# Three passes of 12-bit digits for v in three of the four linear-attention units

## The chip, the cores and the metric

The kernel runs on one core of one Trainium2 (trn2) chip, as one launch. The metric is the device time in microseconds, the median of several runs. Engines are named as the profile names them: PE is TensorE and PEld its weight loads, DVE is VectorE, ACT is ScalarE, POOL is GpSimd, SP is the queue that issues the DMAs.

## The reference, cut to what matters

Two transformer layers on a float32 tensor of 2 x 512 x 256. Only the third of the four blocks is touched:

```python
x = x + _layernorm(_L0_attn_ref(_layernorm(x), ...))   # 16 heads of 128, causal
x = x + _layernorm(_L0_ffn_ref(_layernorm(x), ...))    # 256 -> 2048 -> 256, 4-bit weights
x = x + _layernorm(_L1_attn_ref(_layernorm(x), ...))   # linear attention, below
x = x + _layernorm(_L1_ffn_ref(_layernorm(x), ...))    # 256 -> 688 -> 256, table weights

def _L1_attn_ref(x, W_qkv, W_out):        # D = 256, 16 heads of 16
    q, k, v = split(x @ W_qkv.T, 3)       # x: 2 x 512 x 256
    q, k = elu(q) + 1, elu(k) + 1
    kv_cumsum = cumsum(k * v, axis=sequence)
    k_cumsum = cumsum(k, axis=sequence)
    out = q * kv_cumsum / (q * k_cumsum + 1e-9)
    return out @ W_out.T * 16 ** -0.5
```

Everything is float32, the products on PE too.

## The kernel before, in words

The 1024 rows are four units of 256 rows (`NUNIT`, `TU`). First comes the attention of layer 0, head by head, up to about 384 us of the profile. Then the loop at the end of `sandwich_kernel` writes, for each unit u, the feed-forward block of layer 0: `ffn_hidden(u)` makes eight pairs of hidden chunks, each a gate half (four products into a bank of tag "mm") and an up half (four products into a bank of tag "s"), then a GELU on ACT and a product `hT` on DVE; `ffn_out(u)` multiplies by the down weights. Two halves of unit u+1 are written ahead of `ffn_out(u)`. After the last unit follow `silu_hidden` and `silu_out`, the second feed-forward block, unit by unit.

A product is one call of `matmul`, lines 278 to 286, a 128 x 128 stationary block against 256 moving columns. Since `halved[0]` is set early in the kernel, each call is written as two halves of 64 stationary columns, which run side by side in the array. The hardware runs a float32 half as two instructions (two weight loads and two matmuls in the records), so one call is four matmul records, and each record streams the 256 columns twice.

Beside this main line of PE work run chains: `after_ffn(u)` (norms, then `linear_attention(u)`) is a Python generator that yields a delay and is taken up again by `poll()` when `now[0]`, the planner's own clock of PE, has passed its due time. `poll()` is called after each half of `ffn_hidden` (1.73 us of PE work) and after each two chunks of `ffn_out` (0.86 us). `now[0]` grows by `matmul` calls alone. Each engine's instructions run in the order in which they were written, so the planner decides what stands behind what.

In `linear_attention(u)` the products of k, q and v are written in this order, with a `yield until(f)` after k and after q, so that one half of `ffn_hidden` lies between them. For units 0 to 2 this falls into `ffn_hidden(u + 1)`; unit 3 (`last`) runs inside the second feed-forward block and is on the way to the end.

DVE has filler work: `select_in` builds the down weights `wd` of the second feed-forward block by bit masks and selects, 19 steps a piece. Its steps wait in `vector.fills`; the wrapper `Engine.__getattr__` writes them into gaps that the planner sees in front of another DVE instruction that has to wait for data. `vector.flush()` writes what is left.

Of the kernel before, what the change touches and what calls it, by code (L numbers as in the profile page):

```python
# [10 lines left out]
F32 = mybir.dt.float32  # L11
I32 = mybir.dt.int32
F8 = mybir.dt.float8e4
U8 = mybir.dt.uint8
SIGN = 0x80808080 - (1 << 32)
REST3 = 0x1C1C1C1C
AF = mybir.ActivationFunctionType
ALU = mybir.AluOpType

P = 128  # L20
# [3 lines left out]
D = 256  # L24
NT = S // P
NK = D // P
# [8 lines left out]
TU = HT * P  # L35
NUNIT = B * NT // HT
TURNED = [P, 4, NK, HT, 32]
INTER = 688
NO = -(-INTER // P)
# [151 lines left out]
def sandwich_kernel(  # L191
# [26 lines left out]
    nc = tc.nc  # L218
# [10 lines left out]
    vector, scalar = Engine("DVE", nc.vector, times), Engine("ACT", nc.scalar, times)  # L229
    pool, sync = Engine("POOL", nc.gpsimd, times), Engine("SP", nc.sync, times)  # L230
# [3 lines left out]
    def bank(tag):  # L234
        tile = psum.tile([P, 512], F32, tag=tag, name=f"ps_{tag}")
        used = banks.setdefault(tag, deque(maxlen=2))
        if len(used) == 2:
            times.floor[tile.name] = times.end(used[0])
        used.append(tile.name)
        return tile  # L240
# [36 lines left out]
    def matmul(out, lhsT, rhs, start, stop, beside=False, **more):  # L277
        m = lhsT.shape[-1]
        step = HALF if halved[0] else P
        for at in range(0, m, step):  # L280
            part = slice(at, min(at + step, m))
            nc.tensor.matmul(out[part], lhsT=lhsT[:, part], rhs=rhs, start=start, stop=stop, **more)  # L282
        now[0] = max(now[0], times.start("PE", [out], [lhsT, rhs]))
        if not beside:
            now[0] += (math.prod(rhs.shape[1:]) / 0.6 + 5) / 1e3
        times.add("PE", now[0], [out], [lhsT, rhs])
# [33 lines left out]
    wd = w1.tile([P, NO, D], F32, name="wd")  # L320
# [16 lines left out]
    def chunk(t, kc):  # L337

        return t[:, :, kc].rearrange("p a j t -> p j a t")
# [71 lines left out]
    def norms(u, y, stage, to, eps=EPS, strided=False):  # L411

        x = [xs[u][:, j, :] for j in range(HT)]
        first = [stats(t, eps) for t in y]
        second = []
        for j in range(HT):
            yield until(first[j][0])
            add_scaled(x[j], y[j], first[j][0])  # L420
            second.append(stats(x[j], EPS))
        n = acts.tile([P, HT, D], F32, tag="ln", name=f"ln{stage}_{u}")
        for j in range(HT):
            rstd, shift = second[j]
            yield until(rstd, shift)
            to_n, from_x = n[:, j, :], x[j]
            if strided:
                to_n = to_n.rearrange("p (k m) -> p k m", k=NK)
                from_x = from_x.rearrange("p (m k) -> p k m", k=NK)
            scalar.activation(to_n, from_x, AF.Identity, bias=shift, scale=rstd)  # L430
        yield until(n)
        tr = turning(u, stage)
        for j in range(HT):
            turned_about(tr, n, j)
        brought(to, tr)
        for j in range(HT):
            scalar.activation(x[j], x[j], AF.Identity, bias=first[j][1])

        yield 0.0 if (u, stage) == (2, 1) else until(to)
# [93 lines left out]
    with ExitStack() as at:  # L533
# [257 lines left out]
        def dequantised(packed, scales, u, name, w):  # L791
# [12 lines left out]
            else:  # L804

                for half in range(2):
# [5 lines left out]
                    )  # L812
            p8 = dq.tile([P, UNIT], U8, tag="p8", name="p8")
            c8 = dq.tile([P, 2, UNIT], U8, tag="c8", name="c8")
            two, t = p8.bitcast(I32), pk[:, : UNIT // 4]
# [17 lines left out]
            def values():  # L833
                vector.scalar_tensor_tensor(
                    w,
                    c8.bitcast(F8),
                    64.0,
# [18 lines left out]
        scratch = fh.tile([P, 5, wg.shape[-1]], F32, tag="hT", name="scratch", bufs=1)  # L856
# [275 lines left out]
            yield  # L1132

        def after_ffn(u, po):
            xT2[u] = late["lp"].tile(TURNED, F32, tag="xT2", name=f"xT2_{u}", bufs=1)
            yield from norms(u, [po[:, j * D : (j + 1) * D] for j in range(HT)], 2, xT2[u])
            yield from linear_attention(u)

        xT2, late = {}, {}
# [136 lines left out]
        for rows, cs, base in (  # L1276
# [5 lines left out]
                out=mask[rows, cs],  # L1282
                in_=mask[rows, cs],
# [20 lines left out]
        for i in range(NS + 2):  # L1304
# [5 lines left out]
    lw = late["lw"] = ctx.enter_context(tc.tile_pool(name="lw", bufs=1))  # L1310
    lp = late["lp"] = ctx.enter_context(tc.tile_pool(name="lp", bufs=2))
# [4 lines left out]
    wqkv_sb = lw.tile([P, NK, 3 * D], F32, name="wqkv_sb")  # L1316
# [1 line left out]
    wout_sb = lw.tile([P, NK, D], F32, name="wout_sb")  # L1318
    sync.dma_start(out=wout_sb, in_=wout)
    carry = {}  # L1320
    scratch = lw.tile([P, 8, 2 * D], F32, name="scratch2")
    vector.flush()
    select_in(
        [scratch[:, j] for j in range(8)],
        [
            tuple(t[:, o : o + 2, :].rearrange("p o d -> p (o d)") for t in (down_i, wd))
            for o in range(0, NO, 2)
        ],
    )

    def linear_attention(u):
        def flat(t):
            return t.rearrange("p k t -> p (k t)")

        def project(part, tag):
            ps = bank(tag)
            for ch in range(NK):
                for kc in range(NK):
                    matmul(
                        ps[:, ch * TU : (ch + 1) * TU],  # L1340
                        wqkv_sb[:, kc, part * D + ch * P : part * D + (ch + 1) * P],
                        chunk(xT2[u], kc),
                        kc == 0,
                        kc == NK - 1,
                    )
            return ps

        def of(name, bufs=1):
            return lp.tile([P, NK, TU], F32, tag=name, name=f"{name}_{u}", bufs=bufs)

        k, q, v, ek, eq = of("k"), of("q"), of("v"), of("ek"), of("eq")

        last = u == NUNIT - 1
        for part, e, f in ((1, ek, k), (0, eq, q)):
            ps = project(part, "mm")
            scalar.activation(flat(e), ps, AF.Relu, scale=-1.0)
            scalar.activation(flat(f), ps, AF.Relu)
            if last:

                scalar.activation(e, e, AF.Exp, scale=-1.0)  # L1360
                vector.tensor_scalar(e, e, -1.0, 1.0, ALU.add, ALU.add)
                pool.tensor_add(f, f, e)
            else:
                yield until(f)
        ps = project(2, "s")
        scalar.copy(flat(v), ps)
        if not last:
            for e in (ek, eq):
                scalar.activation(e, e, AF.Exp, scale=-1.0)
            yield until(ek, eq)  # L1370
            for e, f in ((ek, k), (eq, q)):
                vector.tensor_scalar(e, e, -1.0, 1.0, ALU.add, ALU.add)
                pool.tensor_add(f, f, e)
        yield until(k, v)
        ks, kvs, den, lT = of("ks", 2), of("kvs", 2), of("den"), of("lT")

        def running_sum(to, of_):
            for ch in range(NK):
                before = carry[to is kvs, u - 1][:, ch, TU - 1 :] if u % 2 else 0.0
                vector.tensor_tensor_scan(  # L1380
                    to[:, ch, :], ones, of_[:, ch, :], before, ALU.mult, ALU.add
                )
            carry[to is kvs, u] = to

        running_sum(ks, k)
        if not last:
            yield until(ks, q)
        vector.tensor_mul(den, q, ks)
        vector.tensor_scalar(den, den, EPS_LIN, None, ALU.add)
        vector.tensor_mul(v, k, v)  # L1390
        yield until(v)
        running_sum(kvs, v)
        pool.tensor_mul(v, q, kvs)
        yield until(den)
        for ch in range(NK):
            for t in range(HT):
                part = ch, slice(t * P, (t + 1) * P)
                vector.reciprocal(den[:, *part], den[:, *part])
                pool.tensor_mul(lT[:, *part], v[:, *part], den[:, *part])
                yield 0.3  # L1400
        yield until(lT) - 0.8 if last else until(lT) + 0.5
        po = bank("t" if last else "o")
        for t in range(HT):
            for ch in range(NK):
                matmul(
                    po[:, t * D : (t + 1) * D],
                    lT[:, ch, t * P : (t + 1) * P],
                    wout_sb[:, ch, :],
                    ch == 0,
                    ch == NK - 1,  # L1410
                )
        yield 0.3
        t = gp.tile(TURNED, F32, tag="xT3", name=f"xT3_{u}", bufs=4)

        y = [po[:, j * D : (j + 1) * D] for j in range(HT)]
        yield from last_norms(u, y, t, 16 * EPS) if last else norms(u, y, 3, t, 16 * EPS)
        xT3[u] = t
# [221 lines left out]
```

## Time and profile before

| what | value |
|---|---|
| device time, median of 3 runs | 618.01 us (617.85 to 618.13) |
| span of the profiled execution, first to last instruction | 616.7 us |
| what lies around the span in the median of the runs (618.01 - 616.7) | 1.3 us |
| PE busy | 611.1 us, 99%, in 4968 matmul records |
| DVE busy | 486.2 us, 79% |
| ACT busy | 309.3 us, 50% |
| POOL busy | 277.1 us, 45% |
| granted TensorE clock, mean | 0.998 |

A row of the timeline gives the start and the length in us, the engine, the line, the operation, what it writes and reads, the shape and how many records were merged into the row; in brackets the idle time before it and what ended it. All PE rows bear line 282 and most others line 183, since helpers record them; the tiles tell them apart. A matmul record's end is modelled: of its 379 ns some 213 are streaming, so rows overlap, and the time from one row's start to the next row's start is what the stream costs.

### The profile page before, as it was taken

What the parts mean: (1) busy time and instruction counts of PE and PEld (TensorE: products, weight loads), DVE (VectorE), ACT (ScalarE), POOL (GpSimd) and SP (SyncE); (2) the same over time, 40 slices, a digit from 0 to 9 for tenths busy, and PEclk for the clock granted to TensorE, in tenths of its full rate; (3) what the DMA queues carried; (4) which work ended last, traced back from release to release, by engine and by line L of the source; (5) the groups of instructions that cost most, each with busy time, mean ns of one, the idle gap of its engine ahead of it and who ended that gap; (6) DMA issues with size and microseconds to landing.
All of it is one profiled execution on the core that took longest, in us unless ns stands there. A gap on an engine that the chain in (4) does not pass through costs nothing.

```text
span 616.7 us, 13347 instructions
## 1 busy us (share of the span) xinstructions
PE 611.1 (99%) x4968; PEld 470.2 (76%) x4968; DVE 486.2 (79%) x1169; ACT 309.3 (50%) x716; POOL 277.1 (45%) x346
## 2 busy tenths in 40 slices
PE   9999999999999999999999999999999999999996
PEld 7455556566676776767777899999999999996665
DVE  7989988887887999989899789869986751562963
ACT  6657776775666657676566651232324223325210
POOL 5355657454453575855667300350261350161531
PEclk9999999999999999999999999999999999999999
DMA  8477474765647547556552340211001000001010
GB/s 228 137 186 211 107 199 125 171 168 144 158 127 177 168 116 191 152 142 178 113 141 60 84 104 26 98 35 35 1 8 31 1 18 18 1 2 35 19 53 18
DMA packets 44463, 61.43 MB, mean 100 GB/s; under 512 B 5232, under 2 KB 32368, under 8 KB 44400
## 3 DMA queue, kind: packets, MB, share of 16 engines
q1 hardware_dynamic: 44400, 60.59, 38.0%
q8 instruction: 39, 0.64, 0.4%
q14 instruction: 24, 0.20, 0.1%
HBM read 28.59 MB, written 1.05 MB: 48 GB/s over the span
## 4 chain that ended last, share of the span: by engine, by line
PE 98%; DVE 1%; issue 0%; POOL 0%; DVEq 0%
PE ps_mm L282 40%; PE ps_o L282 22%; PE ps_s L282 21%; PE ps_t L282 14%; PE ps_o L579 1%; DVE x L183 0%; DVE p L183 0%; DVE rr L183 0%; DVE ra L183 0%; DVE centred L183 0%; POOL rstd L183 0%; DVE wg L183 0%; PE ps_t L289 0%; DVE st L183 0%; DVE st_last L183 0%
## 5 line engine op out<-in xcount | busy, mean ns | idle before, releaser
L183 DVE SCALAR_TENSOR_TENSOR rr<-ps_mm,cols_sb,sin_sb 64x512 f32<-64x512 f32 (+1 forms) x126 | 93.4, 741 | 3.6 <-PE ps_mm L282 0.7
L183 POOL TENSOR_TENSOR wg<-wg,scratch 128x752 f32<-128x752 f32 x30 | 53.8, 1794 | 89.3 <-DVE scratch L183 86.9
L282 PE MATMUL ps_mm<-xT,wg 128*64 128x256 f32 (+1 forms) x704 | 89.4, 379 | 0.0
L282 PE MATMUL ps_s<-xT,wu 128*64 128x256 f32 x672 | 85.4, 379 | 0.0
L183 ACT ACTIVATE p<-p,mn 128x512 f32<-128x512 f32 (+3 forms) x128 | 70.3, 550 | 27.6 <-DVE mn L183 27.6
L282 PE MATMUL ps_o<-wd,hT 128*64 128x256 f32 (+1 forms) x704 | 77.2, 375 | 0.0
L282 PE MATMUL ps_t<-pT,v 128*64 128x256 f32 (+3 forms) x512 | 76.1, 432 | 0.0
L282 PEld LDWEIGHTS ps_mm<-xT,wg 128*64 128x64 f32 (+1 forms) x704 | 71.7, 137 | 5.5 <-ACT si L183 0.4
L282 PEld LDWEIGHTS ps_o<-wd,hT 128*64 128x64 f32 x704 | 68.9, 137 | 6.2
L282 PEld LDWEIGHTS ps_s<-xT,wu 128*64 128x64 f32 x672 | 69.5, 137 | 4.5 <-DVE hT L183 0.3
L282 PEld LDWEIGHTS ps_t<-pT,v 128*64 128x64 f32 x512 | 49.7, 137 | 27.1 <-issue 19.0
L183 ACT ACTIVATE p<-p,rs 128x512 f32<-128x512 f32 (+3 forms) x128 | 61.4, 551 | 11.2 <-DVE rs L183 9.3
L282 PEld LDWEIGHTS ps_o<-wo,oT 128*64 128x64 f32 x512 | 49.9, 137 | 17.8 <-issue 13.3
L282 PE MATMUL ps_o<-wo,oT 128*64 128x256 f32 x512 | 62.5, 379 | 0.0
L282 PE MATMUL ps_mm<-xT,wq 128*64 128x512 f32 (+2 forms) x256 | 60.5, 577 | 0.1
L282 PE MATMUL ps_mm<-xT,wk 128*64 128x512 f32 x248 | 60.0, 592 | 0.0
L183 POOL TENSOR_TENSOR ra<-ra,cos_sb 128x512 f32<-128x512 f32 (+1 forms) x33 | 41.1, 1245 | 40.2 <-ACT ra L183 38.4
L282 PE MATMUL ps_s<-kT,qT 128*64 128x64 f32 (+5 forms) x384 | 57.0, 424 | 0.0
L282 PE MATMUL ps_mm<-wv,xTv 128*64 128x256 f32 x464 | 56.4, 379 | 0.0
L183 DVE STREAM_TRANSPOSE turned<-p 128x512 f32<-128x512 f32 (+3 forms) x128 | 54.1, 480 | 1.2 <-ACT p L183 0.2
L183 ACT ACTIVATE ln<-x,shift,rstd 128x256 f32<-128x256 f32 x22 | 13.3, 607 | 79.0 <-POOL shift L183 78.2
L282 PEld LDWEIGHTS ps_s<-kT,qT 128*64 128x64 f32 x384 | 34.6, 137 | 23.9 <-issue 11.6
(161 smaller groups left out, 965.3 us busy)
## 6 DMA issues: line engine op xcount, KB each, us to landing
pT<-turned SPq DMA_DIRECT2D x128, 208.0 KB, 3.9
wo<-in_wo SPq DMA_DIRECT2D x17, 256.0 KB, 4.2
wv<-in_wv SPq DMA_DIRECT2D x16, 256.0 KB, 4.2
wq<-in_wq SPq DMA_DIRECT2D x15, 256.0 KB, 4.2
wk<-in_wk SPq DMA_DIRECT2D x15, 256.0 KB, 4.0
xT<-tr SPq DMA_DIRECT2D x48, 64.0 KB, 2.1
pk_g<-in_gate_p SPq DMA_DIRECT2D x4, 256.0 KB, 4.6
sc_g<-in_gate_s SPq DMA_DIRECT2D x8, 128.0 KB, 4.2
```

The lines of the kernel that those rows point to most:

```text
L183: return write(*args, **more)
L282: nc.tensor.matmul(out[part], lhsT=lhsT[:, part], rhs=rhs, start=start, stop=stop, **more)
L579: nc.tensor.matmul(warm[:, :P], lhsT=units, rhs=units, start=True, stop=True)
```

## The change

In units 0 to 2, v's product is no longer four float32 calls but twelve matmuls with operands of type float32r, written straight to `nc.tensor.matmul`, over all 128 stationary columns. The operands are split into digits of 12 bits: x is a high part `top` and a low part, the weights likewise. Pass 0 takes the raw operands (wv3[0], xT2), pass 1 the low parts (the weights' times 4096), and pass 2 the differences. Between pass 1 and pass 2 ACT multiplies the sum in PSUM by 1 + 1/4096; the sum of the three is then the product of the whole numbers. Three DVE instructions per unit make `top`, the low part and the difference of x; four more, `split_weights`, make the weights' parts once, in unit 0. One more DMA copies the raw weights into wv3[0]. Between pass 1 and ACT's multiplication the chain yields 0.5. The bank is of tag "t" where it was "s". To make room, the scratch of `select_in` is halved: the down weights are made in six pieces of 256 columns, where there were three of 512. Unit 3 is as before.

```diff
@@ after_ffn
-            xT2[u] = late["lp"].tile(TURNED, F32, tag="xT2", name=f"xT2_{u}", bufs=1)
+            t = late["lp"].tile(TURNED, F32R, tag="xT2", name=f"xT2_{u}", bufs=1)
+            xT2[u] = t.bitcast(F32)
@@ ahead of linear_attention
-    scratch = lw.tile([P, 8, 2 * D], F32, name="scratch2")
+    scratch = lw.tile([P, 8, D], F32, name="scratch2")
     vector.flush()
     select_in(
         [scratch[:, j] for j in range(8)],
-        [
-            tuple(t[:, o : o + 2, :].rearrange("p o d -> p (o d)") for t in (down_i, wd))
-            for o in range(0, NO, 2)
-        ],
+        [(down_i[:, o, :], wd[:, o, :]) for o in range(0, NO)],
     )
+    wv3 = [lw.tile([P, NK, D], F32R, name=f"wv3_{n}") for n in range(3)]
+    wv_raw = wqkv_sb[:, :, 2 * D :]
+    sync.dma_start(out=wv3[0].bitcast(F32), in_=wv_raw)
+
+    def split_weights():
+        top = lp.tile([P, NK, TU], F32, tag="den", name="top_w", bufs=1)
+        low = lp.tile([P, NK, TU], F32, tag="lT", name="low_w", bufs=1)
+        vector.tensor_scalar(top.bitcast(I32), wv_raw.bitcast(I32), HIGH, None, ALU.bitwise_and)
+        vector.tensor_sub(low, wv_raw, top)
+        vector.tensor_scalar(wv3[1], low, DIGIT, None, ALU.mult)
+        vector.scalar_tensor_tensor(wv3[2], low, -DIGIT, top, ALU.mult, ALU.add)
@@ linear_attention
+        if u == 0:
+            split_weights()
         k, q, v, ek, eq = of("k"), of("q"), of("v"), of("ek"), of("eq")
...
-        ps = project(2, "s")
+        if last:
+            ps = project(2, "s")
+        else:
+            x3 = [xT2[u].bitcast(F32R), *(lp.tile(TURNED, F32R, tag=n, name=f"x{n}_{u}", bufs=1) for n in ("lT", "den"))]
+            top = lp.tile(TURNED, F32, tag="top", name=f"top_{u}", bufs=1)
+            vector.tensor_scalar(top.bitcast(I32), xT2[u].bitcast(I32), HIGH, None, ALU.bitwise_and)
+            vector.tensor_sub(x3[1], xT2[u], top)
+            vector.scalar_tensor_tensor(x3[2], top, -1.0 - 1.0 / DIGIT, xT2[u], ALU.mult, ALU.add)
+            ps = bank("t")
+            for n in (0, 1, 2):
+                if n == 2:
+                    yield 0.5
+                    scalar.mul(ps, ps, 1.0 + 1.0 / DIGIT)
+                for ch in range(NK):
+                    for kc in range(NK):
+                        nc.tensor.matmul(
+                            ps[:, ch * TU : (ch + 1) * TU],
+                            lhsT=wv3[n][:, kc, ch * P : (ch + 1) * P],
+                            rhs=chunk(x3[n], kc),
+                            start=n == 0 and ch == 0 and kc == 0,
+                            stop=n == 2 and kc == NK - 1,
+                            skip_group_check=True,
+                        )
         scalar.copy(flat(v), ps)
```

More of the change, by code (lines that the diff above doesn't have):

```diff
@@ L13 @@
 F8 = mybir.dt.float8e4
+F32R = mybir.dt.float32r
+HIGH = 0xFFFFF000 - (1 << 32)
+DIGIT = 4096.0
 U8 = mybir.dt.uint8
```

## The prediction

> **What bounds the kernel now.** I read the page first: busy shares and the chain that ended last.
>
> ```profile
> PE 611.1 (99%) x4968; PEld 470.2 (76%) x4968; DVE 486.2 (79%) x1169; ACT 309.3 (50%) x716; POOL 277.1 (45%) x346
> ...
> PE 98%; DVE 1%; issue 0%; POOL 0%; DVEq 0%
> ```
>
> PE is busy from end to end and is 98% of the chain. So a microsecond of PE work taken out anywhere is a microsecond of the end, as long as PE stays fed, and a microsecond in which PE waits is one lost. DVE, ACT and POOL matter only where PE would have to wait for them.
>
> Next, the PE timeline around the three changed products (ps_s<-xT,wqkv_sb; the ps_mm rows with wqkv_sb are k and q; wg and wu are gate and up halves of the feed-forward block).
>
> ```profile
> 426.76 2.00 PE L282 MATMUL ps_mm<-xT,wqkv_sb 128*64 128x256 f32 x16
> 428.49 2.01 PE L282 MATMUL ps_mm<-xT,wg 128*64 128x256 f32 x16
> 430.21 2.01 PE L282 MATMUL ps_s<-xT,wqkv_sb 128*64 128x256 f32 x16
> ...
> 471.65 2.01 PE L282 MATMUL ps_s<-xT,wu 128*64 128x256 f32 x16
> 473.38 2.00 PE L282 MATMUL ps_s<-xT,wqkv_sb 128*64 128x256 f32 x16
> 475.11 2.01 PE L282 MATMUL ps_mm<-xT,wg 128*64 128x256 f32 x16
> ...
> 521.73 2.01 PE L282 MATMUL ps_mm<-xT,wg 128*64 128x256 f32 x16
> 523.46 2.00 PE L282 MATMUL ps_s<-xT,wqkv_sb 128*64 128x256 f32 x16
> ```
>
> Two things are to be seen. Each row starts 1.73 us after the one before, with nothing between: v costs 1.73 us per unit today (16 records, 0.108 each). And in units 0 and 2 v stands behind a gate half (wg), in unit 1 behind an up half (wu). That decides below whether the digits are ready.
>
> **Passes removed and added.** Per unit four calls, 1.73 us, go. Twelve matmuls come, each over all 128 columns, in one pass if float32r is what the change takes it for. No row of before has this type. The nearest are the full-width float32 products at the start of the kernel:
>
> ```profile
> 7.48 0.61 PE L282 MATMUL ps_mm<-xT,wq 128*128 128x128 f32 x4
> 7.93 0.60 PE L282 MATMUL ps_o<-xT,wk 128*128 128x256 f32 x2
> 8.36 0.40 PE L289 MATMUL ps_t<-ident,n 128*128 128x128 f32 x2
> 8.60 0.60 PE L282 MATMUL ps_o<-xT,wk 128*128 128x256 f32 x2
> 9.19 0.44 PE L282 MATMUL ps_mm<-xT,wq 128*64 128x256 f32 x2
> ```
>
> A float32 record streams its columns twice. The four of 128 columns (256 streamed) take 0.45 us from 7.48 to 7.93, 0.11 each, with a load of 128 stationary columns hidden under each. Two records of 256 columns take 0.43 from 7.93 to 8.36, 0.215 each. A float32r matmul streams 256 columns once, so I take 0.11: 12 x 0.11 = 1.32 us. The upper end is 0.215, if this type streams twice as well: 2.58 us. Below 0.107, the 256 columns' share of these rows, nothing speaks for it. Gain: 1.73 - 1.32 = 0.41 per unit, 1.2 us in all. This is the most the change can bring: 0.2% of 618.0, which is about what a measurement of this kernel can tell from no change.
>
> **Switching between half and full width.** Every call around is two 64-column halves; the new matmuls take the whole array. Passes 0 and 1 are one block and pass 2, behind the yield, another: two blocks per unit, each with a switch in and one out, 12 switches in all. From full to half there is one row: the second of the two full-width records of the row at 8.60 starts 0.38 before that row's end, at 8.82, and the first half at 9.19. That is 0.37 us where 0.215 is streaming: 0.15 too much, and part of it was a wait for ACT's xT, which ended at 9.13. So this switch costs 0 to 0.15. From half to full no row exists. It lies between 0 (weights load under the last halves, as they do everywhere else) and 0.30: the 0.379 that a half's record lasts in its group less its 0.213 of streaming, 0.17, until the array is empty, and 0.137, the mean of the halves' loads, for a weight load that is no longer hidden. I take 0.10 and 0.15, nearer the middle than the free end, since the one row that has a switch shows a hole: 0.25 a pair, 6 pairs, 1.5 us; ends 0 and 2.7.
>
> The Trainium skill speaks against the change here: "TensorEngine Tiling (Array Packing)", Tiling Modes, says that a change of tiling mode, not of the tile alone, drains the engine. With the load time of "TensorE: Matmul & The Clock Gate", section LDWEIGHTS (columns divided by 1.2, in ns), 107 and 53 ns would be uncovered per pair, an estimate of 1.0 us over six pairs before the emptying itself. No row of before shows a change from half to full.
>
> **The wait of pass 1 for its digits.** Pass 1 needs `top` and the low part from DVE, and stands directly behind pass 0 in PE's queue, so everything on PE waits with it. On DVE the two are queued behind what was written last: the `hT` product of the last up half. Its rows for unit 1:
>
> ```profile
> 473.79 0.69 DVE L183 TENSOR_TENSOR hT<-ge,ps_s 128x512 f32<-128x512 f32 x1 [0.80 <-PE ps_s L282]
> 480.43 0.69 DVE L183 TENSOR_TENSOR hT<-ge,ps_s 128x512 f32<-128x512 f32 x1 [5.96 <-ACT ge L183]
> 481.03 0.42 DVE L183 TENSOR_SCALAR ek<-ek 128x512 f32<-128x512 f32 x1
> 481.37 0.42 DVE L183 TENSOR_SCALAR eq<-eq 128x512 f32<-128x512 f32 x1
> ```
>
> Where v stands behind an up half, hT can start only when that half has ended: 473.79, 0.41 after v could start on PE (473.38). From start to start an hT takes 0.60, an instruction on one tensor of this size 0.34 (481.03 to 481.37) and one on two about that of hT, 0.60. The low part is then there at 473.38 + 0.41 + 0.60 + 0.34 + 0.60 + 0.1 for the semaphore = 475.43. Pass 0 would be done at 473.38 + 0.15 + 0.44 = 473.97. PE waits 1.5 us. Where v stands behind a gate half (units 0 and 2), hT belongs to an up half further back: in unit 0 its row starts at 427.26, the low part is made by 428.9 with the same steps, and v starts at 430.21. That leaves over 1.2 us, in unit 2 (hT at 520.40, v at 523.46) 1.4; there the digits cost nothing.
>
> Does unit 1 keep its place? The chain of unit 0 no longer advances the planner's clock by v's 1.73 us, so later due times move against the halves. I followed the planner's due times by hand: unit 1's k comes due between a gate half and the up half after it, about 0.6 us behind the poll that would turn the order. So I take the order of before for unit 1 (odds two to one) and for unit 2 (three to two), and one wait: 1.5 us; ends 0 and 3.0.
>
> **ACT between passes.** A 512-wide multiplication in PSUM, at most the copy of v (0.59 us). The yield puts a half of 1.73 us on PE between, and ACT's queue there holds one GELU (0.60) that is ready: 1.2 us under 1.73. Nothing on the path. Without that half each unit would lose some 0.7.
>
> **DVE's further work.** Splitting the weights: four instructions, 0.34 + 0.60 + 0.34 + 0.75 (the three-operand rr of 512) = 2.0 us, in the place of filler. Three per unit, 1.7 us. The filler in halved pieces: today 24 steps of 0.54, 12 of 0.41 and 21 of 0.75, 33.6 us; at 256 columns, by the rows of the up weights' pieces (0.43, 0.29 to 0.40, 0.47), 48 x 0.43 + 24 x 0.36 + 42 x 0.47 = 49.0. So 15 us more there and about 22 in all. What hides it:
>
> ```profile
> 437.00:474.00 37.00, 37.00 (x346) 36.92 (x344) 31.56 (x65) 9.42 (x19) 15.97 (x31) 1.00 0.07 16
> 474.00:546.00 72.00, 72.00 (x670) 72.00 (x668) 34.72 (x65) 20.29 (x32) 20.32 (x40) 1.00 0.04 8
> ```
>
> The columns are length, then busy time of PE, PEld, DVE, ACT, POOL. Filler ends at 473 today, and from 474 to 546 DVE has 72 - 34.7 = 37 us free, against the 22. `wd` is read from 559 on. I count 0. If the filler were late in front of an hT that v's digits stand behind, unit 1's wait would grow by up to one step, 0.5.
>
> **SP and the rest.** Four more DMAs on SP, 0.43 each to issue; the copy waits for wqkv (issued at 384.0) and holds what is behind it on SP, the next being turned rows some 10 us later. 0. Unit 3's chain is not touched; its rows land about 0.45 us ahead of their use at 597, so a planner's step lost there could cost 0.4. I keep that for the range.
>
> **The sum.** -1.2 + 1.5 (switches) + 1.5 (one wait) = +1.8 us. The profiled execution would go from 616.7 to 618.5, and with the 1.3 around it the median from 618.0 to 619.8.
>
> **Rivals.** 1. *No wait: v of unit 1 lands behind a gate half.* It takes only a change of one half in the order; against it stand the 0.6 us by hand and today's row at 471.65. -1.2 + 1.5 = +0.3, 618.3: not slower by what can be told. The wait is the whole difference, and decides from about 0.9 us on. 2. *No wait and free switches.* For it: weight loads are hidden everywhere else. -1.2, 616.8. Against it: the hole at 8.82. 3. *Waits in two units*, with unit 2 turned as well: +3.3, 621.3. 4. *The change does not do what it says:* float32r streams twice. Then v takes 12 x 0.215 = 2.58, 0.85 more than today, 2.55 in three units; the switches stay (1.5), and pass 0, longer by 0.42, leaves 1.1 of the wait: +5.2, 623.2. The kernel has no row of the type, so it can't be excluded.
>
> **How the numbers follow.** The forecast 0.40, within itself 618.9 to 621.0; rival 1 0.33; rival 2 0.09; rival 3 0.10; rival 4 0.08. Slower by over 0.2% (619.25): nine tenths of the forecast, rivals 3 and 4, and the upper edge of rival 1 (0.03): 0.58. Faster by over 0.2% (616.77): a little over half of rival 2, whose 616.8 lies on that bound: 0.05. The rest 0.37. The range leaves out rival 4 and most of rival 2: 617.0 to 621.5.
>
> **What would show it.** Matmul rows of 128*128 and 256 columns in float32r, four to a pass, at 0.11 from start to start (0.215: rival 4). Around each block holes of 0.1 to 0.2 us in PE's starts. In unit 1 a hole of about 1.5 us between the first four and the next four, ended by DVE's low part; none in unit 0. Behind the multiplication on ACT no hole. DVE's filler lasting to some 500 us. It would be wrong if the k of unit 1 stands behind a gate half, or if the blocks show no holes at their edges.

## The result: 626.08 us, slower by 1.3%

The changed kernel takes 626.08 us (625.04 to 627.09, four runs), the kernel before 618.02 beside it; the ratio is 1.0129, 95% interval 1.0115 to 1.0143. The prediction was 619.8 with a range of 617.0 to 621.5: the sign is right, the size far off. The four times lie at two levels, 625.04 and 625.27, and 626.88 and 627.09, which turn out to have one cause (see the first experiment). The profiled execution is one of the lower level: 625.27 us, span 623.5. In all runs 1.7 to 1.85 us lie around the span, for the kernel before too (its 13 runs beside the first experiments have spans of 616.0 to 616.8); so the 1.3 that the prediction took from two different executions is no term.

The page of the changed kernel, busy shares and the chain that ended last:

```profile
PE 612.1 (98%) x4956; PEld 388.9 (62%) x4956; DVE 501.4 (80%) x1239; ACT 311.4 (50%) x719; POOL 274.3 (44%) x346
PE 95%; DVE 3%; issue 1%; DMA 0%; POOL 0%; ACT 0%; POOLq 0%; DVEq 0%; ACTq 0%
```

PE's share of the chain fell from 98% to 95% and DVE's rose from 1% to 3%: PE now waits for DVE. The PE timeline, in unit 0 and then in units 1 and 2:

```profile
428.23 1.94 PE L285 MATMUL ps_mm<-xT,wg 128*64 128x256 f32 x16
430.10 0.74 PE L1394 MATMUL ps_t<-xT,wv 128*128 128x256 f32 x4
430.68 0.64 PE L1394 MATMUL ps_t<-xlT,wv 128*128 128x256 f32 x4
431.25 1.95 PE L285 MATMUL ps_s<-xT,wu 128*64 128x256 f32 x16
433.13 0.74 PE L1394 MATMUL ps_t<-xden,wv 128*128 128x256 f32 x4
433.80 1.95 PE L285 MATMUL ps_mm<-xT,wg 128*64 128x256 f32 x16
435.57 1.90 PE L285 MATMUL ps_s<-xT,wu 128*64 128x256 f32 x16
...
473.66 0.74 PE L1394 MATMUL ps_t<-xT,wv 128*128 128x256 f32 x4
475.74 0.74 PE L1394 MATMUL ps_t<-xlT,wv 128*128 128x256 f32 x4 [1.34 <-DVE xlT L186]
...
525.63 1.90 PE L285 MATMUL ps_s<-xT,wu 128*64 128x256 f32 x16
527.45 0.74 PE L1394 MATMUL ps_t<-xT,wv 128*128 128x256 f32 x4
529.45 0.74 PE L1394 MATMUL ps_t<-xlT,wv 128*128 128x256 f32 x4 [1.25 <-DVE xlT L186]
...
595.85 1.03 PE L285 MATMUL ps_o<-wd,hT 128*64 128x256 f32 x8
599.10 4.54 PE L285 MATMUL ps_o<-wd,hT 128*64 128x256 f32 x40 [2.21 <-DVE x L186]
```

In unit 0 nothing waits, and from 428.23 to 435.57 there are three halves and v: 7.34 - 3 x 1.73 = 2.15 us for v, 0.42 more than the 1.73 of before. In unit 1 and also in unit 2 pass 1 stands idle for its digits. In unit 2 the row ahead of v is now an up half (525.63, wu), where it was a gate half before. And near the end there is a hole that no step of the prediction has. DVE's timeline shows what pass 1 waits behind in units 1 and 2, and what stands ahead of the hole:

```profile
473.94 0.68 DVE L186 TENSOR_TENSOR hT<-ge,ps_s 128x512 f32<-128x512 f32 x1
474.54 0.42 DVE L186 TENSOR_SCALAR top<-xT 128x512 int32<-128x512 int32 x1
475.00 0.69 DVE L186 TENSOR_TENSOR xlT<-xT,top 128x512 fp32r<-128x512 f32 x1
...
527.64 0.69 DVE L186 TENSOR_TENSOR hT<-ge,ps_s 128x512 f32<-128x512 f32 x1 [2.31 <-PE ps_s L285]
528.25 0.42 DVE L186 TENSOR_SCALAR top<-xT 128x512 int32<-128x512 int32 x1
528.70 0.69 DVE L186 TENSOR_TENSOR xlT<-xT,top 128x512 fp32r<-128x512 f32 x1
...
595.72 0.45 DVE L186 STREAM_TRANSPOSE tr<-n 128x256 f32<-128x256 f32 x1
596.09 0.65 DVE L186 TENSOR_TENSOR hT<-si,ps_s 128x512 f32<-128x512 f32 x1
...
598.01 0.42 DVE L186 TENSOR_TENSOR hT<-si,ps_mm 48x256 f32<-48x256 f32 x1
598.47 0.48 DVE L186 SCALAR_TENSOR_TENSOR x<-ps_o,rstd,x 128x256 f32<-128x256 f32 x1
```

`hT` reads the up half that has just ended, and the digits queue behind it; pass 1, due at 473.66 + 0.58 = 474.24 (0.58 is the distance in unit 0), starts at 475.74, 1.5 us late; in unit 2 it is due at 528.03 and starts at 529.45, 1.4 us late. The last row ended the wait near the end: `written(1, 1)`, which writes the second half of unit 1's result, reads the second half of `silu_out(1)` out of a bank of `ps_o` only at 598.47, and `silu_out(2)`, which accumulates over both banks of that tag in turn, needs this bank from 596.7 on. In the kernel before, the same read (590.15) came ahead of the last norms' transposes, and `silu_out(1)` ended ahead of unit 3's product with `wout`. DVE and then PE, before:

```profile
590.15 0.47 DVE L183 SCALAR_TENSOR_TENSOR x<-ps_o,rstd,x 128x256 f32<-128x256 f32 x1
590.66 0.35 DVE L183 TENSOR_SCALAR x<-x,shift 128x256 f32<-128x256 f32 x1
590.93 0.41 DVE L183 TENSOR_SCALAR n<-x,mv,rstd 128x256 f32<-128x256 f32 x1
591.37 0.45 DVE L183 STREAM_TRANSPOSE tr<-n 128x256 f32<-128x256 f32 x1
...
578.99 5.35 PE L282 MATMUL ps_o<-wd,hT 128*64 128x256 f32 x48
584.17 1.90 PE L282 MATMUL ps_t<-wout_sb,lT 128*64 128x256 f32 x16
```

and PE in the changed kernel:

```profile
582.90 4.49 PE L285 MATMUL ps_o<-wd,hT 128*64 128x256 f32 x40
587.22 1.90 PE L285 MATMUL ps_t<-wout_sb,lT 128*64 128x256 f32 x16
588.94 1.03 PE L285 MATMUL ps_o<-wd,hT 128*64 128x256 f32 x8
```

Now the product with `wout` stands ahead of the last chunks of `silu_out(1)`, so unit 3's last norms and the hT of silu_hidden(2) are written on DVE first, and the read behind them.

### The profile page after: what moved, and what is told of

It is laid out like the page before. It is cut to its first block, busy times and chain, and to the rows that moved or that the text cites. A ratio compares the mean times of both kernels' runs of the same rounds, so it can differ in the third digit from the quotient of the medians.

```text
span 623.5 us, 13408 instructions
## 1 busy us (share of the span) xinstructions
PE 612.1 (98%) x4956; PEld 388.9 (62%) x4956; DVE 501.4 (80%) x1239; ACT 311.4 (50%) x719; POOL 274.3 (44%) x346
## 4 chain that ended last, share of the span: by engine, by line
PE 95%; DVE 3%; issue 1%; DMA 0%; POOL 0%; ACT 0%; POOLq 0%; DVEq 0%; ACTq 0%
PE ps_mm L285 39%; PE ps_o L285 22%; PE ps_s L285 20%; PE ps_t L285 14%; PE ps_t L1394 1%; DVE scratch L186 1%; DMA x<-in_x_turned 0%; DVE hT L186 0%; DVE wd L186 0%; DVE rr L186 0%; DVE xlT L186 0%; POOL rstd L186 0%; DVE p L186 0%; DVE x L186 0%; DVE st L186 0%
## 5 line engine op out<-in xcount | busy, mean ns | idle before, releaser
L285 PE MATMUL ps_mm<-xT,wg 128*64 128x256 f32 x704 | 86.1, 379 | 0.0
L285 PE MATMUL ps_s<-xT,wu 128*64 128x256 f32 x672 | 82.3, 380 | 0.0
L285 PEld LDWEIGHTS ps_o<-wd,hT 128*64 128x64 f32 x704 | 53.8, 137 | 23.5 <-issue 2.6
L285 PEld LDWEIGHTS ps_mm<-xT,wg 128*64 128x64 f32 x704 | 56.0, 137 | 19.3 <-ACT ge L186 0.2
L285 PEld LDWEIGHTS ps_s<-xT,wu 128*64 128x64 f32 x672 | 53.6, 137 | 18.8 <-DVE hT L186 0.3
L285 PEld LDWEIGHTS ps_t<-pT,v 128*64 128x64 f32 x512 | 40.1, 137 | 36.9 <-issue 28.1
L285 PE MATMUL ps_o<-wo,oT 128*64 128x256 f32 x512 | 61.1, 379 | 0.0
L285 PEld LDWEIGHTS ps_o<-wo,oT 128*64 128x64 f32 x512 | 40.2, 137 | 27.4 <-issue 15.7
L285 PE MATMUL ps_s<-kT,qT 128*64 128x320 f32 (+5 forms) x384 | 57.2, 424 | 0.0
L186 DVE CUSTOM_DVE_ANT_0 p<-ps_s,mask 128x512 f32<-128x512 f32 x64 | 31.2, 488 | 25.2 <-PE ps_s L285 23.8
```

Of the source, the lines that this page charges most:

```text
L186: return write(*args, **more)
```

## The experiments

All are compared with the kernel before on the same chip (618.05 to 618.19 in the median). The changed kernel's lower level is called 625.15, the middle of its two times.

**Digits earlier.**

```diff
+        if not last:
+            x3 = [...]; top = ...       # the three DVE instructions, moved up
         for part, e, f in ((1, ek, k), (0, eq, q)):
             ps = project(part, "mm")
```

> The changed kernel with one thing moved: the three VectorE operations that make xT2's digits (top, xlT, xden) are emitted at the start of the linear attention, ahead of k's product, and no longer behind it. Theory (two digit waits): the rows in which pass 1 starts 1.34 and 1.25 us late for xlT, in units 1 and 2, are gone; pass 1 follows x's high pass after about 0.6 us; the steps stand in the same order, so the late product into ps_o at the tail stays. 626.1 - 2.9 = 623.2, from 622.5 to 624.0. Rival 1 (only unit 1's wait is real, as predicted): 626.1 - 1.5 = 624.6. Rival 2 (the digits are late because xT2 itself is, or they push VectorE's hT rows of the running ffn_hidden, so that the wait moves to other rows): 626.1, within 0.5.

Measured: 623.89 us (621.8 to 624.03), ratio 1.0083 (1.0066 to 1.01). PE's waits view (total us, times, longest) has, in the changed kernel,

```profile
PE ps_t L1394 <- DVE xlT L186: 2.6, 2, 1.3
PE ps_o L285 <- DVE x L186: 2.2, 1, 2.2
```

and here

```profile
PE ps_o L285 <- DVE x L186: 2.2, 1, 2.2
```

Both waits for xlT are gone, the wait for x stays at 2.2. The single run at the lower level, 621.8, is 3.3 below 625.15; the three others, at 623.8 to 624.0, are 3.0 below the upper level. So the two digit waits cost some 3.1 us, and unit 2's was as large as unit 1's: rival 1 of that text, the prediction's own count, is out. This kernel's profile also shows what the two levels are. It was taken on an upper run, and the hole at the end is followed by this, in the windows view (length, busy time of PE, PEld, DVE, ACT, POOL, granted clock, DMA share, GB/s) and the PE timeline:

```profile
594.00:596.00 2.00, 0.06 (x2) 0.09 (x3) 1.42 (x4) 0.64 (x3) 0.00 (x0) 1.00 0.44 95
596.00:597.00 1.00, 1.00 (x7) 0.69 (x9) 0.26 (x1) 0.00 (x0) 0.00 (x0) 0.62 0.32 72
597.00:598.00 1.00, 1.00 (x8) 0.73 (x6) 0.00 (x0) 0.00 (x0) 0.00 (x0) 0.50 0.39 131
598.00:599.00 1.00, 1.00 (x8) 0.71 (x6) 0.00 (x0) 0.00 (x0) 0.00 (x0) 0.50 0.00 0
...
595.95 6.22 PE L285 MATMUL ps_o<-wd,hT 128*64 128x256 f32 x40 [2.21 <-DVE x L186]
```

The clock falls to half for about 3.4 us, and the same 40 records that took 4.54 us in the changed kernel's lower run take 6.22: 1.7 us of the 1.8 between the levels. The idle time in front is 2.21 in both, so the same hole costs 2.2 us in some executions and 3.9 in others: by their times and mean clocks (0.996 against 0.998 and 0.999) the long form came in two of four of the changed kernel and in three of four here; the course of the clock was read in one of each kind.

**The bank, and the order.** Two ways to take the tail's wait away: a bank of another tag, or the product with `wout` later so that the read stands ahead of the last norms again.

```diff
@@ silu_out (first kernel)
-                po[t, cs.start] = bank("t" if cs.start else "o")[:, :D]
+                po[t, cs.start] = bank("t" if cs.start or (u, t) == (NUNIT - 2, 1) else "o")[:, :D]
@@ linear_attention (second kernel)
-        yield until(lT) - 0.8 if last else until(lT) + 0.5
+        yield until(lT) + 0.9 if last else until(lT) + 0.5
```

> The changed kernel with one thing changed: the second accumulation of silu_out(2) takes a PSUM bank of ps_t and no longer one of ps_o, so it need not wait until x has been read out of silu_out(1)'s second half. The order of all steps stays. Theory (tail wait): the 2.21 us of idle TensorE at 596.7, 2.4 from start to start, goes; xT3 of unit 3 is on time for silu_hidden(3), since it was made from operations that ended by 596.2. 626.1 - 2.4 = 623.7; and if the 1.8 us between the changed kernel's two levels (625.2 and 627.0) come from a clock that falls in that idle time, all runs lie at one level, 622.8 (622.4 to 623.3). Rival 1 (the next late thing, xT3 of unit 3, takes the wait's place at silu_hidden(3)): 625 to 626. Rival 2 (the bank is not what was waited for): 626.1.

> The changed kernel with the last unit's product with wout asked for 1.7 us later by the planner's clock (until(lT) + 0.9 for - 0.8). By the planner's order it then stands behind all of silu_out(1) and one step of silu_hidden(2), as it stood behind all of silu_out(1) in the kernel before, and x of silu_out(1)'s second half comes ahead of the last norms' operations in VectorE's queue. Theory (the tail wait is a matter of order in VectorE's queue): the 2.21 us are gone without any change of banks; silu_hidden(3) may wait up to 0.4 for its xT3, which comes some 1.2 us later. 623.7 to 624.1, or 622.8 to 623.3 if the upper of the changed kernel's two levels goes with the idle time. Rival (the bank, not the order): the wait stays, 626.1 or more.

Measured: 622.95 (622.8 to 623.76) with the bank, ratio 1.008 (1.0063 to 1.0097), and 623.39 (622.84 to 623.49) with the order, ratio 1.0081 (1.0066 to 1.0096). In both the row of 2.2 is gone from the waits, the two for xlT stay, and no run lies 1.8 above the others. With the order a hole of 0.18 is left ahead of silu_hidden(3). So the wait is that of a bank, it came from the order in DVE's queue, and the upper level goes with it. What moved the product with `wout` is narrowed by the profiles of the other kernels below. Where v is still written through `matmul` (narrow, wide), it stands behind all 48 records of `silu_out(1)`. Where v's matmuls are written past the planner, it stands behind 40 or 24 of them, unless it is asked for later; so it does in passes_ob too, which leaves out the digits and ACT's multiplication. So neither the longer filler nor the digits' work is needed to move it. The planner's clock, which v's matmuls no longer advance, is the cause that the code suggests; it was not tried by itself. By the times and mean clocks of these eight runs, the digit waits, 1.3 us of idle time each, never took the clock down.

**Filler alone.**

```diff
# in the kernel before
-    scratch = lw.tile([P, 8, 2 * D], F32, name="scratch2")
+    scratch = lw.tile([P, 8, D], F32, name="scratch2")
     # and select_in with (down_i[:, o, :], wd[:, o, :]) for o in range(0, NO)
```

> The kernel before with one part of the change alone: scratch2 of half the width and the fill of wd in pieces of one column block each, twice as many instructions of half the size (some +15 us of VectorE's time). v's product stays in four passes. Theory (the filler is hidden): 618.0, within 0.3; the polls fall a step differently, which is worth a few tenths at most. Rival (a longer filler delays VectorE's hT rows or the norms, and so TensorE, and is part of the 8 us): 619 to 621.

Measured: 618.71 (618.5 to 619.86, ten runs), ratio 1.0011 (1.0002 to 1.0021). Behind the first 6 us PE waits for nothing new. The half microsecond lies behind the last instruction of the engines. Both profiled executions have a span of 616.7, because this one of the kernel before happens to run 0.7 us later from early on (a row at 347.51 stands at 346.82 in narrow, long before the edit); but DVE's last rows are, here and then in the kernel before,

```profile
612.97 0.48 DVE L183 SCALAR_TENSOR_TENSOR x<-centred,rstd_last,x 128x256 f32<-128x256 f32 x1
```

```profile
613.51 0.48 DVE L183 SCALAR_TENSOR_TENSOR x<-centred,rstd_last,x 128x256 f32<-128x256 f32 x1
```

so 3.3 us follow here and 2.7 there. From the last matmul's end to the end of the span it is 5.1 to 5.3 us in all twelve kernels with the narrow filler (the changed one among them), and 4.6 to 4.7 in the two with the wide one. What happens there no row names. One thing differs there: with the narrow filler the DMA view counts 25 to 27 packets of the instruction queue, with the wide one 24, and only with the wide one does the last packet lie a microsecond behind the end of the span. Whether that is the cause no run tests, so it stays open.

**Both repairs, and the price of a block.**

```diff
@@ early_ob: the edits of early and obank
@@ early_ob_one: also
-            ps = bank("t")
+            ps, pd = bank("t"), bank("s")      # pass 2 accumulates in pd, no yield ahead of it
...
-        scalar.copy(flat(v), ps)
+            yield 0.5
+            scalar.mul(flat(v), ps, 1.0 + 1.0 / DIGIT)
+            vector.tensor_add(flat(v), flat(v), pd)
```

> The changed kernel with both repairs: digits emitted ahead of k's product, and silu_out(2)'s second accumulation in a bank of ps_t. Theory (the digit waits and the tail wait are independent and make up all but 1.9 us of the loss): 625.1 (the changed kernel's lower level) - 3.2 (what early took off that level) - 2.3 (what the bank took) = 619.6, from 619.2 to 620.2, in one level; TensorE waits for neither xlT nor x. What is left over the kernel before is the product itself, 3 x 0.42, and the longer filler, 0.6. Rival (the repairs hide each other's gain, because a later wait catches TensorE): 621 or more.

> early_ob with all three passes in one block in each of the three units: the difference pass accumulates in a bank of its own (ps_s), and v is made from the two banks by ScalarE's scaling and a VectorE addition, so that nothing lies between the passes. It saves one pair of mode switches (halves to full width and back) in each unit. Theory (a pair costs 0.36 us, as the starts of the changed kernel's records show): early_ob - 1.1, some 618.5. Prediction's price (0.25 a pair): early_ob - 0.75, some 618.9. Rival (the price lies in the float32r matmuls themselves, not in the switch): early_ob, within 0.2. Rival 2 (VectorE's reading of ps_s holds up the next up product, which takes that bank): early_ob + 0.5 or more.

Measured: 619.82 (619.38 to 620.03), ratio 1.0027 (1.0015 to 1.0038), and 619.90 (619.84 to 620.45), ratio 1.003 (1.0018 to 1.0042). The repairs add up: early_ob's waits view is down to one row, which the kernel before has too:

```profile
PE ps_o L582 <- PEq L1664: 0.8, 1, 0.8
```

The one block brought nothing to the time, against both prices. But behind the first 6 us its profile has two waits that early_ob's lacks, 0.4 and 0.5 us for hT (of unit 0 at 556.7 and of unit 2 at 594.5): the order had changed. To read the block's price without that, TensorE's part was put into the kernel before alone, in two kernels with one order:

```diff
# in the kernel before, with the narrow filler and the ps_t bank of obank
-        ps = project(2, "s")
+            ps = bank("t")
+            for n in (0, 1, 2):
+                if n == 2:
+                    yield 0.5        # passes_one_ob: behind all twelve
+                ...  # four matmuls of 128 columns, wv3[0] and xT2 as float32r
```

> The kernel before with the half-width filler, the ps_t bank for silu_out(2)'s second accumulation, and v's product in three units made of 12 float32r matmuls of full width in two blocks (8, and 4 a step later). The digits are left out: all three passes read x and v's weights as they are, no VectorE digits, no scaling; so it is the price of TensorE's part alone. Theory (0.42 a unit over the four passes: 12 spacings of 0.12 and two pairs of switches of 0.36): narrow's 618.7 + 1.3 = 620.0, and equal to early_ob, since digits that come early enough cost nothing. Prediction's price (12 x 0.11 and two pairs of 0.25, +0.09 a unit): 619.0. Rival (the product gains as its streams suggest, switches free): 617.5.

> passes_ob with the 12 matmuls in one block; the planner's order of all other steps is the same. The digits are left out here as well. Theory (a pair of switches costs 0.36): passes_ob - 1.1. Prediction's price (0.25): passes_ob - 0.75. Rival (no price for the switch, the float32r matmuls are slow): passes_ob, within 0.2.

Measured: 620.99 (620.67 to 621.4), ratio 1.0047 (1.0032 to 1.0061), and 620.15 (619.8 to 620.28), ratio 1.0031 (1.0019 to 1.0043). Both have the two waits for hT, 0.9 us together, so the difference, 0.84, is three pairs of switches: 0.28 a pair, with runs that spread over 0.5 to 0.7 us. Against narrow, passes_ob is 2.28 slower, 0.9 of it these waits, and 1.4 the product: 0.46 a unit, beside the 0.42 of the changed kernel's rows. And 620.99 - 0.9 is early_ob's 619.8 within 0.3: digits that come early cost nothing that can be seen. In the one-block kernel the PE timeline of unit 1 reads:

```profile
471.47 1.90 PE L283 MATMUL ps_s<-xT,wu 128*64 128x256 f32 x16
473.30 1.71 PE L1374 MATMUL ps_t<-xT,wv 128*128 128x256 f32 x12
474.93 1.95 PE L283 MATMUL ps_mm<-xT,wg 128*64 128x256 f32 x16
476.71 1.90 PE L283 MATMUL ps_s<-xT,wu 128*64 128x256 f32 x16
```

From 471.47 to 476.71 two halves and v: 5.24 - 3.46 = 1.78, still 0.05 over the four passes' 1.73. So even with one block in place of two the three passes gain nothing; a unit of two blocks that waits for nothing (early_ob's unit 1, worked out in the same way) takes 2.13, 0.35 more.

**Is it the width or the type?** The kernel before, with v's four passes in float32 at full width.

```diff
+        halved[0] = last
         ps = project(2, "s")
+        halved[0] = True
```

> The kernel before with v's product of units 0 to 2 written as four float32 matmuls of 128 columns in place of eight of 64 (halved off for this call alone): the same four passes, the same bank, the planner's order the same. It asks whether the price of the change's blocks lies in the change of tile width. Theory (a pair of switches costs 0.28 to 0.36 us whatever the type): +0.3 a unit, 618.15 + 0.9 = 619.0. Rival (the price belongs to the float32r type and its own loads): 618.15, within 0.2. Rival 2 (a full-width float32 matmul also shows its loads): 620 or more.

Measured: 619.12 (618.75 to 619.46, eleven runs), ratio 1.0016 (1.0007 to 1.0024): 1.07 over 618.05, 0.36 a pair. So the price does not belong to float32r: leaving half width and coming back costs about a third of a microsecond for float32 as well. The PE timeline of unit 1:

```profile
471.73 1.90 PE L282 MATMUL ps_s<-xT,wu 128*64 128x256 f32 x16
473.56 1.99 PE L282 MATMUL ps_s<-xT,wqkv_sb 128*128 128x256 f32 x8
475.48 1.95 PE L282 MATMUL ps_mm<-xT,wg 128*64 128x256 f32 x16
477.26 1.90 PE L282 MATMUL ps_s<-xT,wu 128*64 128x256 f32 x16
```

1.83 from the up half into the block, 1.92 for the block, 1.78 for the half behind it, each 1.73 without a switch: 0.10, 0.19 and 0.05, in sum 0.34. The middle term is two holes, read from single records: the block's second record starts 0.10 later than streaming asks for, and the half behind the block 0.10 later after the block's last record. At both edges the weight loads do not run ahead: PEld stands idle for 0.39 us ahead of the block's first load, which starts with the block, and for 0.33 ahead of the next half's. "TensorEngine Tiling (Array Packing)" of the Trainium skill, Tiling Modes, says that a change of tiling mode drains the engine. The holes at both edges fit that, though no row shows a drain as such; the runs put 0.28 to 0.36 us on a pair.

**Looking for a better one.** Three more kernels with the one block, each with one delay changed to get rid of the waits for hT: `best` asks for v's scaling at once, one_b and one_c ask for unit 2's product with `wout` later.

```diff
-            yield 0.5                                             # best
             scalar.mul(flat(v), ps, 1.0 + 1.0 / DIGIT)
+            yield 0.5                                             # best
...
-        yield until(lT) - 0.8 if last else until(lT) + 0.5
+        yield until(lT) - 0.8 if last else until(lT) + (1.4 if u == 2 else 0.5)    # one_b; 3.2 in one_c
```

> early_ob_one with ScalarE's scaling of v asked for at once behind the block and not a step later. By the planner's order the last units' steps then fall differently, and VectorE's transposes of unit 3's norms no longer stand ahead of the hT row that TensorE waited 0.9 us for in early_ob_one. Theory (one block is 0.3 to 0.36 us per unit cheaper than two; early_ob_one lost as much by that wait of 0.9): 619.8 - 0.9 = 618.9, or 0.2 to 1.2 over the kernel before, of which 0.15 is the product (12 spacings of 0.12 and one pair of switches, 1.78 against 1.73 us, three times) and the rest the longer filler. Rival (one block saves nothing, or another wait takes the place): 619.8. Rival 2 (the three passes are a gain once nothing waits): 617.5 or less.

> early_ob_one with unit 2's product with wout asked for 0.9 us later by the planner's clock, one step of silu_hidden(0) later, as it stands in early_ob. The three passes in one block stay. Theory (early_ob_one's 0.9 us of waits for hT come only from where that product stands): the two waits go, 619.9 - 0.9 = 619.0. Rival (one block really saves nothing): 619.8.

> The same with that product asked for 2.7 us later, three steps of silu_hidden(0) later. Theory: 619.0 as one_b if no other wait takes the place; unit 3's k then stands nearer to its xT2, by the planner's order at the same step, so a wait of some tenths there is possible. Rival (one block saves nothing): 619.8 or more.

Measured: best 620.33 (619.65 to 620.55), ratio 1.0034 (1.0021 to 1.0048); one_b 620.05 (619.98 to 620.18), ratio 1.0031 (1.0019 to 1.0042); one_c 619.70 (619.16 to 619.92), ratio 1.0024 (1.0015 to 1.0033). In best the waits for hT are gone and one of 1.2 us has come, unit 3's q product for ACT's reading of k; in one_b both waits for hT stay, so where that product stands was not their cause alone; one_c keeps one of 0.46. Less its waits, each lies at 619.1 or 619.2. No version beats the kernel before: the product costs more than it saves, and the order, tuned around products of 1.73 us, has to be found anew for each edit.

## Why the prediction was wrong

The sum left out two waits and priced a term too low: a wait of 1.5 us in unit 2, one of 2.2 us near the end, and switches at 0.25 us a pair.

- **Passes, 12 x 0.11.** Nearly right: the records start 0.117 to 0.122 apart, 1.43 us a unit; one stream per matmul, not two, so rival 4 is out. It missed 0.1 us a unit.
- **Switches, 0.25 a pair.** The mechanism was right, the term too small: 0.28 to 0.36. With the passes this makes the product 0.42 dearer in each unit, where the sum had 0.09: 1.0 us of the miss. It was taken near the middle of its ends, 0 and 0.45 a pair; the measured price lies in the upper half.
- **Wait for the digits.** The mechanism, its place behind hT and its size in unit 1 (1.5 predicted, 1.5 measured) were right; the 0.1 in it for the semaphore was 0.05 (xlT ends at 475.69, pass 1 starts at 475.74). The step that failed is the one on the order in unit 2, "three to two" for no wait: v stood behind an up half there as well. That is rival 3; it costs 1.5 us more. It was given a chance of 0.10, but the two odds, two to one and three to two, make it 2/3 x 2/5 = 0.27 if they are independent. What turned unit 2 stays open: in passes_ob and early_ob_one v stands behind a gate half there, as before.
- **The tail.** "A planner's step lost there could cost 0.4" looked at xT3's rows alone, and the sum had nothing for it. What was late was another thing, a read of a PSUM bank queued on DVE behind the last norms and a later block's hT: 2.2 us, and 1.7 more where the clock fell. This is the largest step that failed, but no single one put the time out of the range. Without the tail wait the kernel takes 622.95 (obank), still above 621.5; without unit 2's 1.5 us as well it would take 621.4 by these numbers.
- **Filler.** Right for PE: nothing was late, though the filler's last instruction is at 524.9, not some 500. Its cost on DVE was put too high: the narrow filler alone adds 7.6 us of busy time (493.8 against 486.2), not 15, and the whole change 15.2, not 22. The 0.5 us at the end of the span was not foreseen.
- **ACT between passes, SP.** Right: no pass waits for either in the changed kernel's profile.

The sum by the runs: product 1.3, digit waits 3.1, tail wait 2.2, end of the span 0.5: 7.1, where 625.15 - 618.02 is 7.1 too; half of the runs have 1.8 on top.

## What to carry to other kernels

Where a planner's clock decides the order, an edit that changes what advances this clock can reorder everything behind it, so list each wait that the order now avoids, PSUM banks among them, not only the ones around the edit. A few full-width matmuls among half-width ones carried a price per block here, not per matmul: put them together, and see whether what they save is more than about a third of a microsecond. Operands that another engine makes from a tile should be asked for where the tile is ready, not where they are used.

## What the runs showed of the hardware

- An idle time of 2.2 us on PE took the granted clock to 0.50 for some 3.4 us in one profile (early) and left it at 1.00 in another (the changed kernel). By times and mean clocks it fell in five of eight executions of these two kernels; with idle times of 1.3 us alone it fell in none of eight (obank, later). "TensorE: Matmul & The Clock Gate" of the Trainium skill, Part 1, gives an idle window of about 3.4 us that runs freely. That the loss differs from run to run is in line with a free-running window; the 2.2 us that were enough here are shorter than the window the page names.
- A float32r matmul of 128 x 128 against 256 columns starts 0.12 us after the one before (the changed kernel); a float32 one of the same shape takes 0.43, two records of 0.216 (wide).
- Some 0.5 us behind the last instruction depend on the filler's width, or on what came with it (three more DMAs and 57 more instructions on DVE); no row says on which.
